# Turning the feed-forward rows in 32x32 blocks on VectorE, by way of DRAM, instead of on TensorE

## The chip, the cores and the metric

The kernel runs on one core of one Trainium2 chip, all in 32-bit floats. The metric is the device time of one execution in microseconds (us), as the median of several runs. TensorE is called PE, its weight loads PEld, VectorE DVE, ScalarE ACT, GpSimd POOL and SyncE SP, as in the profile.

## The reference

The kernel computes one decoder layer on x of [16 batches, 128 tokens, 1024 channels]: a self-attention, a cross-attention on a context, and a gated feed-forward, each on normalised rows and each added to x.

```python
x = x + attn(layernorm(x), Wqkv, bqkv, Wo, bo)            # single head, d = 256
x = x + xattn(layernorm(x), ctx, ctx, Wq, Wk, Wv, Wo, ...)  # 8 heads of 64
Wg, Wu, Wd = (dequantize(...) for each of gate, up, down)  # 4-bit, groups of 64
g = einsum('bsh,ih->bsi', ln, Wg)      # ln = layernorm(x), i < 2752
u = einsum('bsh,ih->bsi', ln, Wu)
x = x + einsum('bsi,hi->bsh', silu(g) * u, Wd)
```

In the feed-forward the contraction runs over the 1024 channels, so TensorE needs the normalised rows turned: channels on the partitions, tokens along the free axis.

## The kernel before

**Stages.** The program runs in four stages that overlap at their borders: the self-attention with the first part of the weight preparation, the cross-attention (one batch after another, batches 8 to 15 and then 0 to 7), the gate and up products with the rest of the weight preparation, and the down products. The products of the feed-forward are Winograd-like: a 2x2 split of tokens, inputs and outputs is done with seven products instead of eight (GATE, DOWN), at two levels for some of them (`two_levels`). The combinations that this needs are made by VectorE (right operands) and GpSimd (left operands).

**Order.** `InOrder` (L54-62) keeps the instructions of an engine in the order in which they are written; `tensor` and `vector` (L529) are such wrappers, so that from the cross-attention on PE and VectorE run in program order, with L62 as the line of all their instructions. ScalarE and the SP queue are ordered by the framework's scheduler, unless a call is wrapped. In the cross-attention, work is put off with `later(n, fn)` and released by `tick()` (L602-612), which is called after each key unit and each query unit: eight ticks to a batch. When the last batch is reached, the ticks go on between the first products of the feed-forward (`beside`, L1502).

**A batch of the cross-attention** (L879-903) is four pairs of a key unit and a query unit. Both fill a PSUM tile kq from a pool of two (`bpk`, L589), which ScalarE's exponential frees for keys (ke, L666) and VectorE's subtraction for queries (qe). The keys' exponentials are already turned in 32x32 blocks by VectorE (kt, L676), written to DRAM (kd, L680) and loaded again with the blocks in place (kh, L684); the product mm<-kh,cxt (L734) reads them as a right operand in runs of 32 values. `project_out` (L789) adds the result to X[b], and `turned(b)` (L771) then normalises the rows for the feed-forward, in two halves n of 512 columns (even and odd channels), into two tiles xn3.

**The turn.** Two ticks later `turn_rows` (L557) turns each half with four 128x128 PE transposes into a PSUM tile tr (pool `btr`, two tiles, shared with the queries' transposes), ScalarE copies it to a tile xt [128, 4, 128], and SP writes xt to DRAM, to `xt_all[pass][n, half]`, laid out [128 partitions, 4 channel groups j, 512 tokens]. Here `half` is which four of a pass's eight batches it is.

**The blocks.** `block_loads` (L541) loads each of the four blocks (n, half) of a pass, [128, 4, 512], in two DMAs of 512 KB, each two j for all tokens. The loads of the first pass are issued by ticks after batch 15 was turned (L783-787), those of the second between products of the feed-forward (L1517). `operand` (L847) and `outer_operand` (L1061) make the combined blocks T[q] from them. A product reads the j-th channel group as `T[q][:, j, :]`, 512 columns without a gap (L1095, L1172); the two-level products read 256 columns of it or of a combination `ti` (L1246-1271, L1326).

Of the kernel before, what the change touches and what calls it, by code (L numbers as in the profile page):

```python
# [11 lines left out]
F32 = mybir.dt.float32  # L12
# [53 lines left out]
def decoder_layer(  # L66
# [467 lines left out]


    PASSES = (HB, 0)
    xt_all = [dram.tile([2, 2, P, JC, TB], F32, name=f"xt{p}", tag=f"xt{p}") for p in range(2)]
    x_all = dram.tile([B, P, C], F32, name="x_all", tag="x_all")
    blocks = {}

    def block_loads(p, blocks):  # L541

        for k in ((0, 0), (1, 0), (1, 1), (0, 1)):
            for i in range(2):
                part = slice(None), ts(i, JC // 2)
                tc.keep_in_program_order(nc.sync.dma_start(blocks[k][part], xt_all[p][k][part]))
                yield

    def new_blocks(pool, tag):

        return {
            (n, half): pool.tile([P, JC, TB], F32, name=f"b{n}{half}", tag=tag(2 * n + half))
            for n in range(2)
            for half in range(2)
        }

    def turn_rows(b, xns, psum, pool):  # L557
        half, i = divmod(b % HB, BPT)
        for n, xn in enumerate(xns):
            tr = psum.tile([P, JC, P], F32, name="tr")  # L560
            for j in range(JC):
                tensor.transpose(tr[:, j, :], xn[:, ts(j, P)], ident)
            xt = pool.tile([P, JC, S], F32, name="xt")
            nc.scalar.copy(xt, tr)
            nc.sync.dma_start(xt_all[PASSES.index(b - b % HB)][n, half][:, :, ts(i, S)], xt)

# [45 lines left out]
    if True:  # L614
# [155 lines left out]

        def turned(b):  # L771

            xns = []
            for n in range(2):
                xn = b2.tile([P, C // 2], F32, name="xn3")

                rows = X[b].rearrange("p (g j e n) -> p n j g e", g=16, j=JC, n=2)[:, n]
                dst = xn.rearrange("p (j g e) -> p j g e", j=JC, g=16)
                normalise_act(dst, rows, b)
                xns.append(xn)  # L780
            nc.gpsimd.dma_start(x_all[b], X[b])
            later(2, lambda: turn_rows(b, xns, btr, b2))
            if b == B - 1:  # L783
                blocks.update(new_blocks(xlate, lambda k: f"X{HB + 2 * k}"))
                loads = block_loads(0, blocks)
                for n in range(8):
                    later(7 + 2 * n, lambda: next(loads))
# [59 lines left out]
        def operand(q):  # L847

            b12 = blocks[0, 1]
            if q == 7:  # L850
                T0[7] = b12
                vector.tensor_tensor(b12, blocks[1, 1], b12, ALU.subtract)
                return
            t = T0[q] = xres.tile(
                [P, JC, TB], F32, name=f"T{q}", tag={5: "X0", 6: "X2", 4: "X4"}[q]
            )
            a, b = {
                5: (b12, blocks[0, 0]),
                6: (blocks[1, 1], T0.get(5)),
                4: (blocks[1, 0], T0.get(6)),  # L860
            }[q]
            vector.tensor_tensor(t, a, b, ALU.subtract)
# [100 lines left out]
    with ExitStack() as gs:  # L963
# [97 lines left out]
        def outer_operand(T, q):  # L1061

            b12 = blocks[0, 1]
            if q == 7:
                vector.tensor_tensor(b12, T[3], b12, ALU.subtract)
                T[7] = b12
                return
            pool, tag = {5: (cxb, "b4"), 6: (xres, "X2"), 4: (xres, "X0")}[q]
            t = T[q] = pool.tile([P, JC, TB], F32, name=f"T{q}", tag=tag)
            a, b = {5: (b12, T[1]), 6: (T[3], T.get(5)), 4: (T[2], T.get(6))}[q]  # L1070
            vector.tensor_tensor(t, a, b, ALU.subtract)

# [2 lines left out]
        def products(T, got, tensor=tensor):  # L1075

            bank, kept = {}, {}

            def keep(q, ps):
                t = kept[q] = ct.tile([P, TB], F32, name="k", tag=f"k{q}", bufs=2 if q == 1 else 1)  # L1080
                nc.scalar.copy(t, ps)

            def product(q):
                wt = next_weights()
                put_stores()
                first = {6: 1, 5: 1, 3: 1, 4: 7}.get(q, q)
                if first == q:
                    banks.rotate(1)
                    bank[q] = banks[0].tile([P, TB], F32, name=f"p{q}", tag="gu")
                ps = bank[first]  # L1090
                for j in range(JC):
                    tensor.matmul(  # L1092
                        ps,
                        wt[:, j, :],
                        T[q][:, j, :],  # L1095
                        start=(first == q and j == 0),
                        stop=(q in (2, 3, 4) and j == JC - 1),
                        skip_group_check=True,
                    )
                if q in (1, 7, 6):  # L1100
                    keep(q, ps)
                elif q == 2:
                    got((0, 0), ps, kept[1])
                elif q == 5:
                    got((1, 1), ps, kept[7])
                elif q == 4:
                    got((1, 0), ps, kept[6])
                elif q == 3:
                    got((0, 1), ps, None)

            return product
# [30 lines left out]
        def last_block(ps, T, between):  # L1142
# [24 lines left out]
            def half_product(p, w, q, start, stop):  # L1167
                for j in range(JC):
                    tensor.matmul(
                        bank[p],  # L1170
                        w[:, j, :],
                        T[q][:, j, :],  # L1172
                        start=(start and j == 0),
                        stop=(stop and j == JC - 1),
                        skip_group_check=True,
                    )
# [57 lines left out]
        class Operands:  # L1234
# [5 lines left out]
            def inner_right(self, q):  # L1240

                R = self.R
                if q in self.kept and (q, 7) in R:
                    return []

                def t(kc, h):  # L1246
                    return self.T[q][:, ts(kc, CHUNKS), ts(h, HT)]

                R[q, 1], R[q, 2], R[q, 3] = t(0, 0), t(1, 0), t(1, 1)

                def comb(k):
                    if k == 7:
                        tag = self.kept.get(q, "ti")
                        pool = {"ti": self.pool, "X4": xres}.get(tag, xlate)
                        R[q] = pool.tile(
                            [P, 4, CHUNKS, HT],
                            F32,
                            name="ti",
                            tag=tag,
                            bufs=1 if self.kept else 2,  # L1260
                        )
                    dst = R[q, k] = R[q][:, (5, 6, 7, 4).index(k)]
                    a, b = {
                        5: (t(0, 1), t(0, 0)),
                        6: (t(1, 1), R.get((q, 5))),
                        7: (t(1, 1), t(0, 1)),
                        4: (t(1, 0), R.get((q, 6))),
                    }[k]
                    vector.tensor_tensor(dst, a, b, ALU.subtract)

                return [lambda k=k: comb(k) for k in (7, 5, 6, 4)]
# [23 lines left out]
        def two_levels(ps, pairs, operands, between=lambda q: None):  # L1295
# [18 lines left out]
            def multiply(n, p):  # L1314
                L, bank = state[n]["L"], state[n]["bank"]
                q = OUTERS[n][1]
                set_ = {6: 1, 5: 1, 3: 1, 4: 7}.get(p, p)
                if set_ == p:
                    bank[p] = banks[n % 2].tile([P, 2, HT], F32, name=f"q{p}", tag="gu")
                dst = bank[set_]  # L1320
                for m in range(2):
                    for c in range(CHUNKS):
                        tensor.matmul(
                            dst[:, m, :],
                            L[p][:, m, c, :],
                            R[q, p][:, c, :],  # L1326

                            start=(set_ == p and m == c == 0),
                            stop=(p in (2, 3, 4) and c == CHUNKS - 1),
                            skip_group_check=True,  # L1330
                        )
                if p in (1, 7, 6):
                    t = state[n]["kept"][p] = ct.tile(
                        [P, 2, HT], F32, name="k", tag=f"k{p}", bufs=2 if p == 1 else 1
                    )
                    scalar.copy(t, dst)
                put_stores()
# [492 lines left out]
```

## Time and profile before

| | |
|---|---|
| time, median of 3 runs | 2290.3 us (2287.9 to 2293.0) |
| time of the profiled execution | 2287.6 us |
| its span in the profile | 2285.8 us |
| busy: PE, DVE, ACT, POOL | 2258.2, 1600.1, 560.0, 471.8 us |
| DMA traffic | 425.23 MB, 270319 packets |
| granted PE clock | 1.00 in all stretches |

By stage, from the view of busy time by stretch (PE, DVE and ACT busy, and the share of the 16 DMA engines):

| us from the span's start | what | PE | DVE | ACT | DMA |
|---|---|---|---|---|---|
| 0 to 252 | self-attention | 241.4 | 197.3 | 37.8 | 0.49 |
| 252 to 806 | cross-attention | 546.5 | 465.6 | 324.4 | 0.62 |
| 806 to 873 | its last batches beside the first products | 66.2 | 22.5 | 36.0 | 0.55 |
| 873 to 1809 | gate and up products | 932.0 | 672.0 | 153.1 | 0.65 |
| 1809 to 2286 | down products | 472.1 | 242.7 | 8.7 | 0.48 |

A line of the groups names the line of the code, the engine, the operation, output<-inputs with their sizes and the count, then the busy time in us and the mean in ns of one, and the idle time of the engine before it. The names are the tiles' names: xn is the normalised rows, tr the PSUM tile of a PE transpose, xt both the turned tile and its place in DRAM, kt and kd the turned keys and their place, kh their load, kq the PSUM tile of key and query units, b a loaded block, T and ti combinations of blocks, w and li left operands, p and q the PSUM tiles of products at one level and at two. In the order of time, a line has its start and its length in us, and in brackets the idle time before it and what ended it. Consecutive matmuls overlap, so that the sum of their lengths is more than the time that they take.

### The profile page before, as it was taken

The page shows a single profiled execution, that of the slowest core. Times are in us where ns is not written, and L with a number is a line of the kernel's source. Part 1 is how long each engine was busy: PE and PEld are TensorE (multiplying, and loading weights), DVE is VectorE, ACT ScalarE, POOL GpSimd, SP SyncE. Part 2 cuts the span into 40 slices and gives each one's busy share as a digit, 9 for nine tenths or more (in the row PEclk, how much of TensorE's full clock was granted, in tenths as well). Part 3 has the DMA queues.
Part 4 walks back from the last instruction along what each step waited for, and adds up shares of the span by engine and source line. Part 5 has one row for each costly group of instructions (what it writes and reads, how often), then busy time and mean ns, then how long its engine had stood idle before and what let it go on. Part 6 is the DMA issues. An engine that isn't in the chain of part 4 may idle for free.

```text
span 2285.8 us, 25587 instructions
## 1 busy us (share of the span) xinstructions
PE 2258.2 (99%) x9096; PEld 1612.5 (71%) x9096; DVE 1600.1 (70%) x2145; ACT 560.0 (24%) x893; POOL 471.8 (21%) x381
## 2 busy tenths in 40 slices
PE   8999999999999999999999999999999999999999
PEld 7556566666666664444584468888888588888888
DVE  6997788788788937666696658877777555544463
ACT  2111255665665652111111111121111100000000
POOL 5452122222222210000240024444443000000000
PEclk9999999999999999999999999999999999999999
DMA  6445366566676558877747942654554974434631
GB/s 246 158 135 182 102 166 183 158 194 185 173 230 196 169 165 269 276 261 262 242 137 232 322 137 95 202 185 139 192 196 137 331 242 151 142 124 149 222 116 37
DMA packets 270319, 425.23 MB, mean 186 GB/s; under 512 B 26224, under 2 KB 119792, under 8 KB 270064
## 3 DMA queue, kind: packets, MB, share of 16 engines
q1 hardware_dynamic: 244112, 377.71, 52.3%
q0 software_dynamic: 8064, 27.27, 3.2%
q10 hardware_dynamic: 18016, 18.62, 2.6%
q8 instruction: 73, 1.20, 0.2%
q14 instruction: 54, 0.44, 0.1%
HBM read 265.62 MB, written 157.35 MB: 185 GB/s over the span
## 4 chain that ended last, share of the span: by engine, by line
PE 91%; DVE 5%; issue 1%; DMA 1%; ACT 1%; POOL 0%; SPq 0%; DVEq 0%; POOLq 0%; ACTq 0%
PE po L1715 21%; PE q L62 20%; PE p L62 18%; PE mm L62 11%; PE kq L62 9%; PE mm L391 4%; PE tr L62 3%; PE mm L406 2%; PE p L1092 2%; DVE pa L62 1%; PE mm L287 1%; PE tr L338 1%; DVE ti L62 0%; DVE bnst L62 0%; DMA kh<-kd 0%
## 5 line engine op out<-in xcount | busy, mean ns | idle before, releaser
L62 PE MATMUL p<-b,w 128*128 128x512 f32 x560 | 246.4, 592 | 0.0
L62 PE MATMUL q<-ti,li 128*128 128x256 f32 x1008 | 232.2, 379 | 3.5 <-DVE ti L62 3.4
L62 PEld LDWEIGHTS q<-ti,li 128*128 128x128 f32 x1008 | 191.0, 190 | 31.3 <-issue 2.8
L62 POOL TENSOR_TENSOR li<-w 128x512 f32<-128x512 f32 x84 | 117.8, 1405 | 432.2 <-DMA w<-wu 244.4
L62 PEld LDWEIGHTS p<-b,w 128*128 128x128 f32 x560 | 106.4, 190 | 133.1 <-issue 129.4
L1715 PE MATMUL po<-wc,lc 128*128 128x256 f32 x840 | 183.4, 379 | 0.0
L62 PE MATMUL p<-T,w 128*128 128x512 f32 x400 | 177.2, 592 | 0.0
L709 POOL TENSOR_TENSOR qe<-qe,qden 128x1024 f32<-128x1024 f32 x64 | 121.7, 1901 | 266.5 <-DVE qden L62 244.7
L1715 PEld LDWEIGHTS po<-wc,lc 128*128 128x128 f32 x840 | 159.6, 190 | 21.8
L62 ACT COPY k<-q 128x512 f32<-128x512 f32 x126 | 73.7, 585 | 400.0 <-PE q L62 400.0
L62 PEld LDWEIGHTS p<-T,w 128*128 128x128 f32 x400 | 76.0, 190 | 95.7 <-issue 94.9
L1715 PE MATMUL po<-wq,lq 128*128 128x256 f32 x560 | 126.7, 379 | 0.4 <-issue 0.4
L62 PE MATMUL mm<-kh,cxt 128*128 128x256 f32 x512 | 122.6, 382 | 3.2 <-DMA kh<-kd 2.8
L62 PEld LDWEIGHTS mm<-qs,m_sb 128*128 128x128 f32 x512 | 97.2, 190 | 38.9 <-issue 28.0
L62 PE MATMUL kq<-cx,wk_sb 128*128 128x512 f32 x256 | 120.7, 594 | 3.5 <-ACT ke L666 3.5
L62 DVE TENSOR_REDUCE qmx<-kq 128x16 f32<-128x1024 f32 x64 | 76.3, 1193 | 63.8 <-PE kq L62 63.8
L62 PE MATMUL kq<-wq_sb,xn 128*128 128x512 f32 x256 | 120.4, 593 | 0.0
L62 PE MATMUL mm<-qs,m_sb 128*128 128x256 f32 x512 | 120.3, 379 | 0.0
L62 PEld LDWEIGHTS mm<-kh,cxt 128*128 128x128 f32 x512 | 95.9, 190 | 33.5 <-issue 19.1
L1715 PEld LDWEIGHTS po<-wq,lq 128*128 128x128 f32 x560 | 106.0, 190 | 16.0 <-issue 1.0
L62 DVE TENSOR_TENSOR pa<-pa,sz 128x1024 f32<-128x1024 int32 x86 | 114.6, 1333 | 2.5
L391 PE MATMUL mm<-xnT,wqkv_sb 128*128 128x512 f32 (+1 forms) x320 | 113.4, 511 | 0.0
(193 smaller groups left out, 3886.1 us busy)
## 6 DMA issues: line engine op xcount, KB each, us to landing
w<-wu SPq DMA_DIRECT2D x140, 256.0 KB, 3.1
lq<-h SPq DMA_DIRECT2D x140, 256.0 KB, 4.3
w<-wg SPq DMA_DIRECT2D x138, 256.0 KB, 2.8
kd<-kt SPq DMA_DIRECT2D x64, 512.0 KB, 3.5
kh<-kd SPq DMA_DIRECT2D x128, 256.0 KB, 5.6
h<-hc SPq DMA_DIRECT2D x80, 256.0 KB, 2.8
wq<-wd SPq DMA_DIRECT2D x70, 256.0 KB, 5.0
h<-h SPq DMA_DIRECT2D x60, 256.0 KB, 2.5
```

The lines of the kernel that those rows point to most:

```text
L62: return lambda *args, **kw: self._tc.keep_in_program_order(fn(*args, **kw))
L287: tensor.matmul(ps, oT[:, d, ts(b % BPT, S)], wo_d[d][:, ts(h, 512)], start=(d == 0), stop=(d == 1),)
L338: nc.tensor.transpose(tr[:, j, :], xn[:, ts(4 * h + j, P)], ident)
L391: nc.tensor.matmul(ps[:, tokens], wqkv_sb[:, f, c, :], xnT[:, c, tokens], start=(c == 0), stop=(c == CC - 1),)
L406: nc.tensor.matmul(ps, xnT[:, c, ts(i, S)], wqkv_sb[:, 4:6, c, :], start=(c == 0), stop=(c == CC - 1),)
L709: nc.gpsimd.tensor_tensor(qe, qe, den.unsqueeze(2).to_broadcast(wide), ALU.mult)
L1092: tensor.matmul(ps, wt[:, j, :], T[q][:, j, :], start=(first == q and j == 0), stop=(q in (2, 3, 4) and j == JC - 1), skip_group_check=True,)
L1715: nc.tensor.matmul(bank[:, i, :], l[:, ts(i, S)], w,  start=(start and c == 0 and i % 2 == 0), stop=(stop and c == len(pairs) - 1), skip_g ...
```

## The change

The 16 calls of `turn_rows` no longer use PE and ScalarE. The normalised rows of a batch go into one tile xn3 [128, 8, 128] (both halves n), VectorE turns it with one instruction in 32x32 blocks into a tile xt of [128, 4, 8, 32], and four DMAs, one for each group of 32 partitions, write it to DRAM; block c of the rows' columns belongs on partitions 32c to 32c+31, which the DMA from DRAM brings about. `xt_all` has another layout: by batch, token group a, column block c, partition i, and then contiguous (n, j, 32 tokens).

A block is now [128, 16 token groups, 4 channel groups j, 32 tokens] instead of [128, 4, 512]. Its loads are still two of 512 KB, each now eight token groups with all four j, in contiguous pieces of (j, 32 tokens). All that reads a block or a combination, at one level and at two, takes the j-th channel group as 16 (or 8) runs of 32 tokens.

```diff
     PASSES = (HB, 0)
-    xt_all = [dram.tile([2, 2, P, JC, TB], F32, name=f"xt{p}", tag=f"xt{p}") for p in range(2)]
+    xt_all = [
+        dram.tile([HB, 4, 4, Q, 2, JC, Q], F32, name=f"xt{p}", tag=f"xt{p}") for p in range(2)
+    ]
...
+    TOKENS = TB // Q
...
     def block_loads(p, blocks):
-        for k in ((0, 0), (1, 0), (1, 1), (0, 1)):
+        for n, half in ((0, 0), (1, 0), (1, 1), (0, 1)):
             for i in range(2):
-                part = slice(None), ts(i, JC // 2)
-                tc.keep_in_program_order(nc.sync.dma_start(blocks[k][part], xt_all[p][k][part]))
+                src = xt_all[p][ds(half * BPT + 2 * i, 2), :, :, :, n]
+                tc.keep_in_program_order(
+                    nc.sync.dma_start(
+                        blocks[n, half][:, ts(i, TOKENS // 2)],
+                        src.rearrange("b a c i j t -> (c i) (b a) j t"),
+                    )
+                )
                 yield
     def new_blocks(pool, tag):
         return {
-            (n, half): pool.tile([P, JC, TB], F32, name=f"b{n}{half}", tag=tag(2 * n + half))
+            (n, half): pool.tile([P, TOKENS, JC, Q], F32, name=f"b{n}{half}", tag=tag(2 * n + half))
...
-    def turn_rows(b, xns, psum, pool):
-        half, i = divmod(b % HB, BPT)
-        for n, xn in enumerate(xns):
-            tr = psum.tile([P, JC, P], F32, name="tr")
-            for j in range(JC):
-                tensor.transpose(tr[:, j, :], xn[:, ts(j, P)], ident)
-            xt = pool.tile([P, JC, S], F32, name="xt")
-            nc.scalar.copy(xt, tr)
-            nc.sync.dma_start(xt_all[PASSES.index(b - b % HB)][n, half][:, :, ts(i, S)], xt)
+    def turn_rows(b, xn, pool):
+        kt = pool.tile([P, 4, 2 * JC, Q], F32, name="xt")
+        vector.transpose(
+            kt.rearrange("p c m t -> p m c t"), xn.rearrange("p m (c i) -> p m c i", c=4)
+        )
+        xt = xt_all[PASSES.index(b - b % HB)][b % HB]
+        for a in range(4):
+            nc.sync.dma_start(
+                xt[a].rearrange("c i n j t -> i c (n j t)"),
+                kt[ts(a, Q)].rearrange("i c m t -> i c (m t)"),
+            )
...
         def turned(b):
-            xns = []
+            xn = b1.tile([P, 2 * JC, P], F32, name="xn3")
             for n in range(2):
-                xn = b2.tile([P, C // 2], F32, name="xn3")
                 rows = X[b].rearrange("p (g j e n) -> p n j g e", g=16, j=JC, n=2)[:, n]
-                dst = xn.rearrange("p (j g e) -> p j g e", j=JC, g=16)
+                dst = xn[:, ts(n, JC)].rearrange("p j (g e) -> p j g e", g=16)
                 normalise_act(dst, rows, b)
-                xns.append(xn)
             nc.gpsimd.dma_start(x_all[b], X[b])
-            later(2, lambda: turn_rows(b, xns, btr, b2))
+            later(2, lambda: turn_rows(b, xn, b1))
...
-                [P, JC, TB], F32, name=f"T{q}", tag={5: "X0", 6: "X2", 4: "X4"}[q]
+                [P, TOKENS, JC, Q], F32, name=f"T{q}", tag={5: "X0", 6: "X2", 4: "X4"}[q]
...
-                        T[q][:, j, :],
+                        T[q][:, :, j],
...
-                    return self.T[q][:, ts(kc, CHUNKS), ts(h, HT)]
+                    return self.T[q][:, ts(h, HT // Q), ts(kc, CHUNKS)]
...
-                            [P, 4, CHUNKS, HT],
+                            [P, 4, HT // Q, CHUNKS, Q],
...
-                            R[q, p][:, c, :],
+                            R[q, p][:, :, c],
```

The line `T[q][:, :, j]` stands in both kinds of one-level product, and the tile of `outer_operand` has the same new shape.

More of the change, by code (lines that the diff above doesn't have):

```diff
@@ L1068, in outer_operand @@
             pool, tag = {5: (cxb, "b4"), 6: (xres, "X2"), 4: (xres, "X0")}[q]
-            t = T[q] = pool.tile([P, JC, TB], F32, name=f"T{q}", tag=tag)
+            t = T[q] = pool.tile([P, TOKENS, JC, Q], F32, name=f"T{q}", tag=tag)
             a, b = {5: (b12, T[1]), 6: (T[3], T.get(5)), 4: (T[2], T.get(6))}[q]
@@ L1171, in half_product @@
                         w[:, j, :],
-                        T[q][:, j, :],
+                        T[q][:, :, j],
                         start=(start and j == 0),
```

## The prediction, made before the changed kernel was run

> **What bounds the kernel now.** I read the busy shares and the chain of waits first, to learn which engine sets the end:
>
> ```profile
> PE 2258.2 (99%) x9096; PEld 1612.5 (71%) x9096; DVE 1600.1 (70%) x2145; ACT 560.0 (24%) x893; POOL 471.8 (21%) x381
> PE 91%; DVE 5%; issue 1%; DMA 1%; ACT 1%; POOL 0%; SPq 0%; DVEq 0%; POOLq 0%; ACTq 0%
> ```
>
> TensorE (PE) holds 91% of the chain. A busy PE isn't one at its peak, so next come the stretches in which the change works: one period of the cross-attention, a fuller one, and the stretch where the second half's blocks are loaded.
>
> ```profile
> 425.00:460.00 35.00, 35.00 (x158) 24.04 (x157) 29.12 (x36) 21.48 (x37) 8.79 (x6) 1.00 0.62 179
> 740.00:775.00 35.00, 35.00 (x160) 24.04 (x159) 33.00 (x37) 21.34 (x34) 8.79 (x6) 1.00 0.61 178
> 1220.00:1310.00 90.00, 90.00 (x211) 39.77 (x211) 56.42 (x80) 10.79 (x19) 0.00 (x0) 1.00 1.00 305
> ```
>
> (Columns: PE, PEld, DVE, ACT, POOL busy, granted clock, DMA share, GB/s.) PE has no gap in any of them; VectorE has 5.9 us of 35 free in the first, 2.0 in the second; the DMA engines are full in the third. Then the groups removed or to be copied from:
>
> ```profile
> L62 PE MATMUL tr<-ident,xn 128*128 128x128 f32 x128 | 16.8, 273 | 0.1
> L564 ACT COPY xt<-tr 128x512 f32<-128x512 f32 x32 | 18.4, 584 | 1.0
> L62 DVE STREAM_TRANSPOSE kt<-ke 128x1024 f32<-128x1024 f32 x64 | 79.2, 1237 | 0.0
> ```
>
> Last, the order of time around one turn:
>
> ```profile
> 506.79 1.89 PE L62 MATMUL mm<-qs,m_sb 128*128 128x256 f32 x8
> 508.51 1.89 PE L62 MATMUL mm<-kh,cxt 128*128 128x256 f32 x8
> ...
> 512.83 1.89 PE L62 MATMUL mm<-kh,cxt 128*128 128x256 f32 x8
> ...
> 514.29 1.23 DVE L62 TENSOR_TENSOR qe<-kq,qmx 128x1024 f32<-128x1024 f32 x1
> ...
> 514.56 1.04 PE L62 MATMUL tr<-ident,xn 128*128 128x128 f32 x8
> ...
> 515.43 1.88 PE L62 MATMUL kq<-cx,wk_sb 128*128 128x512 f32 x4
> 515.43 1.24 DVE L62 STREAM_TRANSPOSE kt<-ke 128x1024 f32<-128x1024 f32 x1
> ...
> 517.35 1.22 DVE L62 TENSOR_REDUCE knmax<-kq 128x1 f32<-128x1024 f32 x1 [0.68 <-PE kq L62]
> ...
> 521.66 1.23 DVE L62 TENSOR_REDUCE qmx<-kq 128x16 f32<-128x1024 f32 x1 [1.67 <-PE kq L62]
> ```
>
> Durations overlap on PE, so its price is from start to start: the eight transposes hold it from 514.56 to 515.43, 0.87 us, or 0.109 us each, not the 273 ns of the group. VectorE's two gaps end when PE delivers.
>
> **What the skill says.** (1) "TensorE: Matmul & The Clock Gate", Part 4: PE-mode transpose: some 275 ns in a kernel's context, and a copy out of PSUM after. The record here agrees (273 ns), but the spacing is 109 ns; I use the spacing. (2) "VectorE: DVE Perf Modes", The three transpose paths: VectorE turns 32x32 blocks only, within SBUF. Hence the way through DRAM. Our trace has the operation, at 1.237 us for 128x1024. (3) "SBUF — State Buffer", Who interferes with whom: a VectorE instruction with one SBUF input, outside the two-port modes, doesn't contend with GpSimd. The 64 key transposes of before agree: 1233 to 1246 ns, whatever GpSimd does beside them. (4) "DMA: Bandwidth & Descriptors", Specifications: line rate from 512 B on. The trace roughly agrees: xt<-xt writes 512 B runs, 256 KB landing in 2.9 us, beside 2.8 to 3.1 us for the w loads with 2 KB runs.
>
> **The change part by part.**
>
> *Removed from PE:* 8 transposes x 16 batches = 128 x 0.109 = 13.9 us. They lie in stretches where PE has no gap, so all of it is on the path: -13.9.
>
> *Removed from ScalarE:* 32 copies x 0.584 = 18.7 us. ScalarE is 61% busy in the period (21.48 of 35), behind PE: 0.
>
> *Added on VectorE:* 16 transposes x 1.237 = 19.8 us. Per period its work goes from 29.1 to 30.4 us while the period shrinks from 34.86 (515.43 less 480.57, the same product a batch earlier) to 33.99. It fits, but VectorE runs in program order, so I follow the tick. The new transpose would run after qe, from 515.5 to 516.7, and the key transpose to 518.0. knmax then starts 0.6 us later than before, ScalarE's exponential ends near 520.4, and with it the PSUM buffer of this key unit comes free. The key unit that reuses it is two units on, at 524.4 (489.55 plus a period), now 523.5: 3 us of slack. By the next qmx (now due at 520.8) VectorE has caught up, since the gap of 1.67 us absorbs the rest. Cost 0 in 15 batches. In the batch with two T operands VectorE has 33.0+1.24 = 34.2 us in 34: I put 0.3 us on it; ends 0 and 1.2 (the whole transpose shows).
>
> *New waits:* the transpose waits for ScalarE's normalised rows on VectorE, and knmax, qden and the next qmx queue behind it; those rows are made two ticks ahead (504.15 to 505.7 for a turn at 514.6), so nothing is waited for. One xn3 and one xt buffer instead of two half-size ones: each is reused a batch later, tens of us. The SP queue waits for VectorE instead of ScalarE.
>
> *SP queue:* four stores per batch instead of two, 2 x 0.52 = 1.04 us more, behind a transpose that ends 1 us or so after the last copy did. The key store (517.81) queues behind and slips by up to 2 us; its loads come 12 us later (530.3). Cost 0.
>
> *DMA:* two windows give a price by packet size: 320 to 600 us, 36059 packets, 46.13 MB, 58.4% of 16 engines = 72.6 ns at 1279 B; 1216 to 1310, 13679 packets, 28.49 MB, 99.2% = 109 ns at 2083 B. So an estimate of 14.6 ns + 45 ns per 1000 B: 38 ns for 512 B, 200 ns for 4 KB. A block load of 512 KB had 128 pieces of 4 KB, 1.6 us on 16 engines; with 1024 pieces of 512 B it is 2.4. The stores gain: 1 KB pieces, half as many. The 8 loads of the first half are issued from 641 to 702 us, and the first use of the last is at 720, so they have time; but one kh load there already holds PE for 2.6 us. The 8 loads of the second half (1216 to 1290) add 8 x 0.8 = 6.5 us of work where the share is 1.00. PE doesn't wait for DMA there: weights are asked for four tiles, about 13.8 us of products, ahead and land in 5 to 7. But VectorE's weight preparation does (one wait of 8.0 us for a store). Bounds: -2.6 (the kh stall goes) to +6.5; I take +0.5.
>
> *Right operands by blocks of 32 tokens:* the product reads runs of 32 values, 128 B, with a stride. 1072 products of 512 columns and 2352 of 256 do so; in passes of 256 that is 4496. The trace has the case: mm<-kh,cxt reads runs of 32 too, and eight take 1.73 us (512.83 to 514.56) against 1.72 for the contiguous mm<-qs,m_sb (506.79 to 508.51). Cost 0; the upper end is 0.01/8 = 1.25 ns per pass, 5.6 us. A gain is excluded, as contiguous already runs at the full spacing. VectorE's combinations of these operands keep their element counts; kt<-ke writes runs of 32 at the speed of a contiguous 128x1024 (1.22 to 1.23): 0.
>
> *Sum:* -13.9 + 0.3 + 0.5 = -13.1. On the profiled execution (span 2285.8, 2287.6 with what lies around) 2274.5; the median of the runs, 2290.3, lies 2.7 above it, so 2277.2; I say 2277.
>
> **What is next.** PE stays the bound. In the fuller period VectorE is level with it, and a further VectorE task there would show.
>
> **The rivals.**
> (a) *The gain is partly given back to the DMA engines.* For: share 1.00 from 1220 to 1310, 0.82 around 690 with a kh stall. Against: no PE wait at 1.00. The 6.5 us in full, after 0.3 elsewhere: 2290.3 - 13.9 + 6.8 = 2283.
> (b) *VectorE's order becomes the bound in the cross-attention.* If each transpose pushed PE by 0.87 or more per batch, the gain is gone: 2290. For: 30.4 of 34 us, in order, with waits on PE in between. Against: 740 to 775, where 33.0 of 35 on VectorE left PE without a gap.
> (c) *Slower: strided reads of the right operand.* Should PE read runs of 32 more slowly with 16 runs than with 8, each pass pays. It decides from 13.9 / 4496 = 3.1 ns per pass, 1.4% of 0.216 us; at 6 ns it is 27 us, 2303. For: the means of the two groups stand at 382 and 379 ns. Against: their medians are both 379, and the spacing.
> (d) *PE's time in the tail doesn't follow*, because the transposes there fill waits for ScalarE; three of 16 batches, 2.6 us: inside the range.
>
> **How the numbers follow.** Likeliest (full gain) 0.72, (a) 0.14, (b) 0.07, (c) 0.07. The likeliest's own range is 2272 to 2281 (the kh stall gone or VectorE's and part of the DMA cost). For 8 in 10 the range takes in (a): 2272 to 2287; (b), (c) and some of the low end stay out. About 0.2%, 4.6 us, can be told from no change here: faster means below 2285.7. That is the likeliest, and most of (a): 0.83; same: (b) and a rest of (a), 0.09; slower: (c) and a little of (b), 0.08.
>
> **What would show it.** Right: period of the cross-attention 34.0 us from one kq<-cx to the same a batch on; tr<-ident,xn and xt<-tr gone; VectorE near 30.4 per period; p and q product spacing as before (0.43 and 0.216 us). Wrong: PE waits for ke or qe between 320 and 800 (b); PE or VectorE waits on DMA growing at 690 or 1220 to 1310 (a); q<-ti,li or p<-T,w means above 379 and 592 ns (c). Unequal order on the SP queue could shift single stalls by some us either way.

## The result, and the profile after

| | before | after |
|---|---|---|
| median of the runs | 2289.1 us (4 runs) | 2273.2 us (2272.05 to 2274.74, 4 runs) |
| ratio to before | 1 | 0.9927 [0.9914, 0.9939] |
| profiled execution, its span | 2287.6, 2285.8 us | 2272.22, 2270.4 us |
| busy: PE, DVE, ACT, POOL | 2258.2, 1600.1, 560.0, 471.8 us | 2243.3, 1616.5, 546.2, 473.7 us |

The change is faster by 0.7%. On 2290 us the ratio is 16.7 us, between 14.0 and 19.7; my sum was 13.1 and the forecast 2277. In a later session it came to 0.9924 [0.9911, 0.9936].

The page of the changed kernel, engines and chain of waits:

```profile
PE 2243.3 (99%) x8968; PEld 1598.7 (70%) x8968; DVE 1616.5 (71%) x2161; ACT 546.2 (24%) x861; POOL 473.7 (21%) x381
PE 91%; DVE 6%; issue 2%; DMA 1%; ACT 1%; POOL 0%; SPq 0%; DVEq 0%; POOLq 0%; ACTq 0%
```

PE lost 14.9 us of busy time and is still 91% of the chain: the bound hasn't moved. Now the stretches (the columns are those of the prediction). The first line is one whole period of the cross-attention, from a key unit's first product to the same product a batch later; the second is the fullest one, in which VectorE also makes two T operands; the third is where the second half's blocks are loaded. Then the period of before.

```profile
477.26:511.25 33.99, 33.99 (x150) 23.07 (x149) 29.99 (x36) 20.50 (x32) 8.79 (x6) 1.00 0.67 190
724.15:758.14 33.99, 33.99 (x150) 23.08 (x148) 32.87 (x35) 20.34 (x32) 7.74 (x6) 1.00 0.63 186
1200.00:1320.00 120.00, 120.00 (x281) 53.03 (x280) 80.76 (x107) 15.37 (x26) 1.21 (x1) 1.00 0.92 280
```

```profile
480.57:515.43 34.86, 34.86 (x158) 23.90 (x157) 28.98 (x35) 21.32 (x35) 8.78 (x6) 1.00 0.61 181
```

PE is busy through all of them. VectorE has 30.0 us of work in a period of 33.99 (29.0 of 34.86 before, the last line, between the starts that the prediction names), and in the fullest 32.9 of 33.99. The DMA share in the third is 0.92 over the whole 120 us, and no PE gap goes with it. The groups:

```profile
L62 PE MATMUL p<-b,w 128*128 128x512 f32 x560 | 246.4, 592 | 0.0
L62 PE MATMUL q<-ti,li 128*128 128x256 f32 x1008 | 232.2, 379 | 3.5 <-DVE ti L62 2.8 <-ACT k L62 0.6
L62 DVE STREAM_TRANSPOSE kt<-ke 128x1024 f32<-128x1024 f32 x64 | 78.7, 1230 | 0.3 <-issue 0.3
L62 DVE STREAM_TRANSPOSE xt<-xn 128x1024 f32<-128x1024 f32 x16 | 19.8, 1234 | 1.0 <-ACT xn L147 1.0
```

`tr<-ident,xn` and `xt<-tr` are gone; in their place stand 16 VectorE transposes at 1234 ns. The products that now read runs of 32 tokens still take 592 and 379 ns, as these lines of before have it:

```profile
L62 PE MATMUL p<-b,w 128*128 128x512 f32 x560 | 246.4, 592 | 0.0
L62 PE MATMUL q<-ti,li 128*128 128x256 f32 x1008 | 232.2, 379 | 3.5 <-DVE ti L62 3.4
```

Their spacing is the old one too: between the 201st and the 561st product of 512 columns the traces have 154.50 us in both kernels. The order of time around a turn:

```profile
477.26 1.88 PE L62 MATMUL kq<-cx,wk_sb 128*128 128x512 f32 x4
...
511.25 1.88 PE L62 MATMUL kq<-cx,wk_sb 128*128 128x512 f32 x4
...
512.12 1.23 DVE L62 STREAM_TRANSPOSE xt<-xn 128x1024 f32<-128x1024 f32 x1
...
513.28 1.20 DVE L62 STREAM_TRANSPOSE kt<-ke 128x1024 f32<-128x1024 f32 x1
...
514.41 1.18 DVE L62 TENSOR_REDUCE knmax<-kq 128x1 f32<-128x1024 f32 x1
...
517.47 1.23 DVE L62 TENSOR_REDUCE qmx<-kq 128x16 f32<-128x1024 f32 x1 [0.47 <-PE kq L62]
```

From the first line to the second is one batch: 33.99 us. The lines of before had 480.57 to 515.43, 34.86. VectorE does the new turn at 512.12, then the keys', and knmax starts 3.2 us after the key unit's first product, 1.9 us before. By the next qmx it has caught up: its gap there is 0.47 us instead of 1.67. This is the tick as I had followed it. (The prediction's 0.6 us for knmax is on the clock of before; from a key unit that itself starts 0.87 us sooner that is 1.5 us later, and 1.2 was measured.)

One long wait is gone that the sum took as likely to stay. PE's waits for the load kh, in total us, times and longest, before and after:

```profile
PE mm L62 <- DMA kh<-kd: 2.8, 2, 2.6
```

```profile
PE mm L62 <- DMA kh<-kd: 0.2, 1, 0.2
```

The wait of 2.6 us is gone; the 0.2 that is left, at 302 us, is in both. The reason is the subject of experiment 3.

### The profile page after: what moved, and what is told of

It is laid out like the page before. It is cut to its first block, busy times and chain, and to the rows that moved or that the text cites. A ratio compares the mean times of both kernels' runs of the same rounds, so it can differ in the third digit from the quotient of the medians.

```text
span 2270.4 us, 25324 instructions
## 1 busy us (share of the span) xinstructions
PE 2243.3 (99%) x8968; PEld 1598.7 (70%) x8968; DVE 1616.5 (71%) x2161; ACT 546.2 (24%) x861; POOL 473.7 (21%) x381
## 4 chain that ended last, share of the span: by engine, by line
PE 91%; DVE 6%; issue 2%; DMA 1%; ACT 1%; POOL 0%; SPq 0%; DVEq 0%; POOLq 0%; ACTq 0%
PE po L1725 21%; PE q L62 20%; PE p L62 18%; PE mm L62 11%; PE kq L62 8%; PE mm L391 4%; PE tr L62 2%; PE p L1102 2%; PE mm L406 2%; DVE pa L62 1%; PE mm L287 1%; PE tr L338 1%; DVE ti L62 0%; DVE bnst L62 0%; DVE kt L62 0%
```

## The experiments

All ratios are to the kernel before, timed in turn with it on the same chip. The changed kernel stands at 0.9927, and at 0.9924 in a later session.

**1. PE's turns put back.** The changed kernel, with the eight transposes of each batch also on PE, into a PSUM tile that nobody reads.

```diff
     def turn_rows(b, xn, pool):
         kt = pool.tile([P, 4, 2 * JC, Q], F32, name="xt")
+        for n in range(2):
+            tr = btr.tile([P, JC, P], F32, name="tr")
+            for j in range(JC):
+                tensor.transpose(tr[:, j, :], xn[:, JC * n + j], ident)
         vector.transpose(
```

> The changed kernel with the eight 128x128 PE transposes of each batch put back beside VectorE's (their PSUM tile is read by nobody; no ScalarE copy). My theory (the gain is PE's spacing, 0.109 us a transpose, on a path without gaps): 128 x 0.109 = 13.9 us more than the changed kernel, 2273.2 + 13.9 = 2287, and a period of the cross-attention of 34.86 us instead of 33.98. Rival 1 (the gain comes from ScalarE's copies and its freer queue, or from the other DMA sizes): within 3 us of the changed kernel, 2273 to 2276. Rival 2 (PE pays the 273 ns of the record): 35 us more, 2308.

Measured: 2286.3 us, 0.9984 [0.9977, 0.9992]. That is 0.0057 to 0.0060 above the changed kernel, 13.1 to 13.7 us, with some 3.5 us of uncertainty from the two intervals. The period, from a key unit's first product to the next batch's:

```profile
482.67 1.88 PE L62 MATMUL kq<-cx,wk_sb 128*128 128x512 f32 x4
...
517.53 1.88 PE L62 MATMUL kq<-cx,wk_sb 128*128 128x512 f32 x4
```

34.86 us, the period of before to 0.01 us. So eight transposes take 0.87 us of PE, and neither the copies that ScalarE no longer does nor the other stores have a part in it, for here too the copies are away and the stores are the new ones. The 273 ns of the record would have made 35 us. But this kernel is still faster than before by 0.8 to 2.3 parts in a thousand: something else had been gained.

**2. The layout alone.** The turn as before, on PE and ScalarE, with the blocks, their loads and the right operands of the changed kernel.

```diff
-        kt = pool.tile([P, 4, 2 * JC, Q], F32, name="xt")
-        vector.transpose(
-            kt.rearrange("p c m t -> p m c t"), xn.rearrange("p m (c i) -> p m c i", c=4)
-        )
+        kt = pool.tile([P, 4, 2, JC, Q], F32, name="xt")
+        for n in range(2):
+            tr = btr.tile([P, JC, P], F32, name="tr")
+            for j in range(JC):
+                tensor.transpose(tr[:, j, :], xn[:, JC * n + j], ident)
+            nc.scalar.copy(kt[:, :, n].rearrange("p a j t -> p j a t"),
+                           tr.rearrange("p j (a t) -> p j a t", a=4))
         for a in range(4):
-            nc.sync.dma_start(xt[a].rearrange("c i n j t -> i c (n j t)"), ...)
+            nc.sync.dma_start(xt[a].rearrange("c i n j t -> (c i) (n j t)"), ...)
```

> The turn as before (eight PE transposes, ScalarE's copies), with the new layout of blocks in DRAM and SBUF, its loads in pieces of 512 B, its four stores a batch and the right operands in runs of 32 tokens. My theory: the layout costs PE nothing; means of the product groups stay at 592 and 379 ns, time as the kernel before within 3 us (2286 to 2290, the lower end if the one kh stall of 2.6 us goes). Rival (c) of the prediction (strided reads cost PE): 2295 or more with a wider spacing of the products. Rival (a) (pieces of 512 B cost): up to 6.5 us more, 2292 to 2296, with PE or VectorE waiting on DMA from 1220 to 1320 us.

Measured: 2290.6 us, 0.9999 [0.9991, 1.0007]. No cost to within 2 us, and the groups say the same:

```profile
L62 PE MATMUL p<-b,w 128*128 128x512 f32 x560 | 246.4, 592 | 0.0
L62 PE MATMUL q<-ti,li 128*128 128x256 f32 x1008 | 233.7, 381 | 3.5 <-DVE ti L62 2.8 <-ACT k L62 0.6
```

Runs of 32 tokens, 128 B, are read at the speed of a contiguous operand, also when there are 16 of them. The slower rival (c) is refuted. In this run a kh wait of 2.0 us is still there: the layout isn't what took it away.

**3. One cxt load moved.** In the kernel before, the scheduler had put the load of a context tile ahead of four kh loads on the SP queue:

```profile
689.07 0.33 SPq L654 DMA_DIRECT2D cxt<-in_cxt  x1
689.51 1.80 SPq L684 DMA_DIRECT2D kh<-kd  x4
...
699.53 1.97 PE L62 MATMUL mm<-kh,cxt 128*128 128x256 f32 x8 [2.56 <-DMA kh<-kd]
```

The waits of the SP queue name what held it:

```profile
SPq L654 <- PE mm L62: 6.6, 1, 6.6
```

The cxt load couldn't start until PE had read a buffer, and held the queue 6.6 us for it; kh came 2.56 us too late for PE. In the changed kernel's queue, cxt stands behind kh there:

```profile
677.74 1.75 SPq L696 DMA_DIRECT2D kh<-kd  x4
...
693.27 0.93 SPq L666 DMA_DIRECT2D cxt<-in_cxt  x1
```

The edit gives the kernel before this order. The traces show what else moved with it: one block load, which stood at 701.83 ahead of the next four kh loads, now stands behind them as in the changed kernel, and ScalarE makes one copy xt<-tr 2.4 us earlier, at 726. Both come after the stall. All else on the SP queue, PE, VectorE and GpSimd has the same order.

```diff
-            nc.sync.dma_start(ct, cxt[b])
+            d = nc.sync.dma_start(ct, cxt[b])
+            if b == 6:
+                tc.keep_in_program_order(d)
...
-                        nc.sync.dma_start(
-                            t[ts(c, Q)], kd[:, :, c].rearrange("p i o n j -> i p o n j")
-                        )
+                        tc.keep_in_program_order(nc.sync.dma_start(...))
```

> The kernel before with one load of the SP queue moved: the context tile cxt of batch 6 is issued behind the four kh loads that it stood ahead of, nothing else. My theory (the 2.6 us by which the change beat my forecast are this one stall, made by the scheduler's order of the SP queue and not by the change's own work): the PE wait of 2.56 us on kh at 697 us goes and the time falls by 2.6, to 0.9989 of the kernel before. Rival (the stall is made by the DMA engines' load around 690, whatever the order): the wait stays, no change of time.

Measured: 2286.1 us, 0.9982 [0.9976, 0.9989], 4.1 us less (2.5 to 5.5), with 21 runs against 45. The wait:

```profile
PE mm L62 <- DMA kh<-kd: 0.4, 1, 0.4
```

The wait of 2.6 us is gone, as expected (the 0.4 is another, at 304 us, which the kernel before has with 0.2). The middle of the timed gain is 1.5 us more, and the granted clock fits it. Over the 45 runs of the kernel before it has a mean of 0.9985, over these 21 runs 0.9994, and 0.0009 of 2286 us is 2 us. The two kernels that keep the stall, before and experiment 2, both have 0.9985; experiments 1 and 3 and the changed kernel, which lack it, have 0.9994 to 0.9995. (The versions of experiments 4 to 6, which wait longer at the border to the feed-forward, lie between 0.9980 and 0.9990.) Compared at the same listed clock, this version is 2.3 to 2.8 us faster, which is the wait. The split is an estimate from the clocks listed for the runs; that the stall brings the lower clock about isn't shown by a run of its own. The trace of experiment 2 shows how the two may hang together. There PE's wait for kh ends at 699.21, after 2.0 us, and then comes a stretch at half clock:

```profile
699.65:703.05 3.40, 3.40 (x9) 2.40 (x8) 2.28 (x3) 0.23 (x1) 0.00 (x0) 0.50 1.11 367
```

3.4 us at half the clock are 1.7 us of work lost. It doesn't follow every such wait: the profiled execution of the kernel before went on at 1.00 after its 2.56 us. (The profiled execution here has a span of 2285.6 us, only 0.2 below the one of before, because it started the cross-attention 0.8 us later and had 3.4 us at half clock from 1202.5, behind another PE wait of 2.4 us, where the one of before had none.)

The remainder of experiment 1 is the same size: it too has the changed kernel's order. Experiment 2 has the old one, so it is the new turn, and not the layout, that the scheduler answered with another order. So the change's gain has two parts, 13 to 14 us of PE work and some 4 us of queue order with what follows from it; together about 17.5, beside the 16.7 measured.

**4. More turns on VectorE.** The changed kernel, with each batch's transpose done twice, or four times, into the same tile:

```diff
-        vector.transpose(
-            kt.rearrange("p c m t -> p m c t"), xn.rearrange("p m (c i) -> p m c i", c=4)
-        )
+        for _ in range(2):  # 4 in the second
+            vector.transpose(
+                kt.rearrange("p c m t -> p m c t"), xn.rearrange("p m (c i) -> p m c i", c=4)
+            )
```

> The changed kernel with VectorE's transpose of each batch done twice into the same tile (16 x 1.234 = 19.7 us more on VectorE). My theory: VectorE has 31.6 of 33.98 us in a period, still fits, and PE doesn't wait: the changed kernel within 2 us, 2273 to 2275. Rival (b) of the prediction (VectorE's order binds in the cross-attention already): each of 16 turns shows, 2285 to 2293.

Measured: 2277.9 us, 0.9944 [0.9932, 0.9957]: 3.9 us above the changed kernel, though the intervals touch. The expected upper end was 2. A period:

```profile
476.72:510.71 33.99, 33.99 (x150) 23.03 (x149) 31.17 (x37) 20.61 (x32) 8.78 (x6) 1.00 0.67 193
```

33.99 us as before, with VectorE at 31.2: in the steady stretch another 1.2 us cost nothing, so my theory holds there. The excess lies at the late end of the cross-attention: PE waits 4.8 us for ke instead of 3.7, the new gaps being at 766 and 775 us, behind a period with two T operands in which VectorE was busy for 33.4 of 33.99 us; and it waits 3.0 for the first weights w<-wg instead of 1.7. Behind this last wait stand 3.4 us at half clock, from 797.3, which neither profiled execution of the changed kernel has.

> The changed kernel with VectorE's transpose of each batch done four times into the same tile (16 x 3 x 1.234 = 59 us more on VectorE). My theory: VectorE's work in a period is 30.4 + 3.7 = 34.1 us, more than PE's 33.98, and it still has a gap or two waiting on PE, so that here it becomes the bound: a period of 34.5 to 36 us, 8 to 30 us more than the changed kernel, 2281 to 2303, with PE waiting for ScalarE's ke. If VectorE had hidden slack (rival: its program order costs nothing at all until the sum is over the period) only 2 us: 2275.

Measured: 2308.3 us, 1.0081 [1.0067, 1.0094], 35 us above the changed kernel, more than expected. A period, and PE's wait over the whole run:

```profile
475.24:511.38 36.14, 34.79 (x149) 22.80 (x149) 33.58 (x39) 20.79 (x33) 8.78 (x6) 1.00 0.60 172
```

```profile
PE kq L62 <- ACT ke L679: 20.7, 28, 1.6
```

The period is 36.14 us, 2.15 more. VectorE is busy for 33.6 of it, 93%, and PE has gaps that end with ke. So rival (b) is a real mechanism, at a load that the change doesn't reach: the changed kernel is at 30.0 of 33.99, 88%. The share alone doesn't set the point: experiment 6 runs at 94%, batch after batch, with no PE gap. Here all four transposes lie in one piece of 5.07 us ahead of the keys' transpose and knmax, and knmax starts 7.0 us after its key unit's first product, where the changed kernel has 3.2: 3.8 us later, against the 3 us of slack that the prediction counted for the PSUM tile. And VectorE, in program order, still waits for PE once in the period (1.9 us for qmx). Whether the long piece or the sum of the work sets the period wasn't separated.

**5. Loads of 4 KB again.** The changed kernel with `xt_all` laid out [pass][n, half, partition, batch, token group, j, 32]: loads in pieces of 4 KB, eight stores a batch in pieces of 512 B.

```diff
-        dram.tile([HB, 4, 4, Q, 2, JC, Q], F32, ...)
+        dram.tile([2, 2, P, BPT, 4, JC, Q], F32, ...)
...
-                src = xt_all[p][ds(half * BPT + 2 * i, 2), :, :, :, n]
+                src = xt_all[p][n, half, :, ds(2 * i, 2)]
...
         for a in range(4):
-            nc.sync.dma_start(
-                xt[a].rearrange("c i n j t -> i c (n j t)"),
-                kt[ts(a, Q)].rearrange("i c m t -> i c (m t)"),
-            )
+            for n in range(2):
+                nc.sync.dma_start(
+                    xt[n, half, :, i, a].rearrange("(c i) j t -> i c (j t)", c=4),
+                    kt[ts(a, Q), :, ts(n, JC)].rearrange("i c m t -> i c (m t)"),
+                )
```

> The changed kernel with another layout of the turned rows in DRAM: the block loads read pieces of 4 KB again, and the stores write pieces of 512 B (eight of them a batch instead of four). SBUF and the products stay as in the changed kernel. My theory: the pieces of 512 B cost some 6 us of DMA work from 1200 to 1320 us and nothing on the path, so the time stays within 2 us of the changed kernel (2271 to 2275) while the DMA share in that stretch falls. Rival (a) (they cost on the path): 3 to 6.5 us faster than the changed kernel.

Measured: 2276.7 us, 0.9941 [0.9927, 0.9955]: not faster than the changed kernel, rather 3 us slower, with intervals that overlap. Rival (a) is refuted: nothing was waiting on the pieces of 512 B. The stretch of the block loads:

```profile
1200.00:1320.00 120.00, 120.00 (x281) 53.19 (x280) 79.77 (x109) 16.23 (x27) 0.00 (x0) 1.00 0.91 276
```

A share of 0.91 where the changed kernel has 0.92. I had expected it to fall by some 6 us of 120, which is 0.05. My price by packet size was wrong at its upper end. In the packet records of these two traces, from 1200 to 1320 us, a piece of 512 B takes 34 ns on average, near my 38, but one of 4 KB takes 272 to 281, where I had 200; eight small ones cost as much as one large one. A block load lands after 6.3 us in the median in both, as before the change.

That this version isn't as fast as the changed one is mostly the granted clock: it has a mean of 0.9984 over the five runs, against 0.9995 and 0.9994, which is some 2.4 us. Its profiled execution, 2.0 us longer than the changed kernel's, has 3.4 us at half clock from 253.6, ahead of all that the edit touches. Why the clock was lower in these runs stays open.

**6. The same trick once more.** With 4 us of VectorE free in a steady period, one of the four query units of a batch can be turned that way too: one VectorE transpose, four stores, and a load two ticks later, in the layout of `xt`; the product reads `qs` in runs of 32. First in all batches, then in the third to eleventh, then in the third to thirteenth.

```diff
+            def turn_by_dram():
+                qd = dram.tile([4, 4, Q, 8 * Q], F32, name="qd", tag="qd", bufs=2)
+                qt = bqs.tile([P, 4, 2, 4, Q], F32, name="qs", tag="qs")
+                qs.append(qt.rearrange("p a i r t -> p r i a t"))
+                kt = bkt.tile([P, 4, NB, Q], F32, name="kt")
+                vector.transpose(kt.rearrange("p c m t -> p m c t"),
+                    qe.rearrange("p h d -> p (h d)").rearrange("p (m c y) -> p m c y", c=4, y=Q))
+                for a in range(4):
+                    nc.sync.dma_start(qd[a].rearrange("c y x -> y c x"),
+                                      kt[ts(a, Q)].rearrange("y c m t -> y c (m t)"))
+                later(2, lambda: nc.sync.dma_start(qt.rearrange("p a i r t -> p a (i r t)"),
+                                                   qd.rearrange("a c y x -> (c y) a x")))
...
-            later(4, turn)
+            later(4, turn_by_dram if by_dram else turn)
```

Here `by_dram` is pair 0 of every batch in the first version, and pair 0 of the batches named in the two others.

> The changed kernel, in which one of a batch's four query units is also turned by VectorE in 32x32 blocks and by way of DRAM (one transpose, four stores, one load), instead of by eight PE transposes and two ScalarE copies. It takes another 128 transposes from PE: -13.9 us. VectorE then has 31.6 us in a period of 33.1. The run with one more vector turn came out 3.9 us above the changed kernel, so some of it shows: I expect 4 to 8 us back, 2263 to 2269, faster than the changed kernel. Rival (VectorE's order binds, or kh loads now wait behind the new stores on the SP queue): 2273 or more, with PE waiting for ke, kh or qs.

Measured: 2270.2 us, 0.9913 [0.99, 0.9925], 3 us below the changed kernel, though the intervals overlap: less than expected. Where the other 11 of 13.9 us went is seen by stretch. First the changed kernel, its start and the border to the feed-forward, then this one, with a period between:

```profile
252.00:320.00 68.00, 63.03 (x227) 34.19 (x225) 60.38 (x76) 29.49 (x44) 15.52 (x11) 1.00 0.46 130
785.00:806.00 21.00, 19.34 (x87) 12.50 (x86) 18.02 (x21) 10.66 (x17) 6.04 (x6) 1.00 0.85 245
```

```profile
252.00:320.00 68.00, 59.16 (x196) 30.30 (x195) 60.74 (x76) 27.75 (x40) 15.50 (x11) 1.00 0.56 163
466.74:499.85 33.11, 33.11 (x141) 22.25 (x140) 31.11 (x37) 19.62 (x31) 8.77 (x7) 1.00 0.78 223
785.00:806.00 21.00, 17.97 (x59) 11.58 (x60) 10.00 (x12) 5.51 (x10) 3.01 (x3) 0.84 0.93 283
```

The period is 33.11 us, 0.88 less again, with VectorE at 31.1 (94% of it): in the middle the trick pays in full. But PE has 59.2 us of work in the first 68, where it had 63.0; the third batch starts at 318.8 us instead of 316.3, although 1.7 us of transposes are gone from the two ahead of it, and VectorE still has the last of the self-attention there. And at the border PE has 18.0 of 21, at a granted clock of 0.84: a wait of 3.7 us for the first weights, which ends at 788.0, and 6.8 us at half clock, from 786.6. Hence the second version:

> As the run with one query unit by DRAM, but only in the third to eleventh of the 16 batches, where VectorE has the room; in the first two (which also finish the self-attention) and in the last five (block loads, T operands, the border to the feed-forward) the unit is turned on PE as in the changed kernel. Where the loss of the full version lay at the two ends (my theory), the nine units give their 9 x 8 x 0.109 = 7.8 us in full: 2265 where the changed kernel has 2273. Where the loss is spread over all batches (rival), about half of the full version's gain: 2271 or more.

Measured: 2265.8 us, 0.9891 [0.9876, 0.9906], 7.0 us below the changed kernel in the same session; 7.8 was the full gain of nine units. The rival's 2271 is excluded: the loss lay at the ends.

> The same in the third to thirteenth batch: two more units in the batches that also load the blocks, 9.6 us less than the changed kernel if they too come free: 2263.6; 1 to 3 us more than that if the loads from 640 to 705 us then hold up kh (theory), so 2264 to 2267.

Measured: 2264.8 us, 0.9888 [0.9874, 0.9901]; 8.0 us below the changed kernel, of 9.6. The stretches:

```profile
252.00:320.00 68.00, 62.02 (x218) 33.30 (x216) 59.68 (x75) 29.85 (x44) 15.50 (x11) 1.00 0.45 132
640.00:705.00 65.00, 65.00 (x282) 43.88 (x281) 61.33 (x72) 39.82 (x61) 16.57 (x12) 1.00 1.00 277
785.00:806.00 21.00, 20.30 (x70) 13.10 (x70) 10.16 (x12) 6.59 (x11) 3.01 (x3) 0.92 0.86 262
```

The start is nearly that of the changed kernel again, and PE has no gap from 640 to 705 although the DMA share there is 1.00. The 0.92 at the border is 3.4 us at half clock from 786.4, behind a PE wait of 1.9 us for the first weights that ends at 785.7. This is the fastest kernel of the study. It can't be told from the version with nine units.

> The changed kernel once more, beside the two others and the kernel before on one chip, so that the differences of a few us have a base: 0.993 of the kernel before.

Measured: 2272.8 us, 0.9924 [0.9911, 0.9936].

## Why the prediction was right

*Removed from PE, -13.9.* Right. Experiment 1 gives 13.1 to 13.7, with 3.5 us of uncertainty, and the period is 0.87 us shorter. What made it right is taking the spacing (0.109 us) and not the record (0.273), and having read that PE has no gap where the transposes lay.

*Removed from ScalarE, 0.* Right: in experiment 1 ScalarE's copies stay away and the period is that of before.

*Added on VectorE, 0.3.* Right in size: no PE gap in the period or in the fullest one, and one new gap of 0.18 us behind it, at 774.0, that ends with ke. Experiment 4 shows how near the edge is: a second transpose is free in the steady batches, and three more aren't.

*New waits, SP queue, 0.* Right in the cross-attention. The four stores don't even take the 1.04 us more that I had counted: 1.75 us of the queue, where the two of before took 1.95. But one wait at the border was put at nothing without a reason: PE waits 1.7 us for the first weights, w<-wg, in both executions of the changed kernel, and 0.7 before and 0.8 in experiment 1, where it still makes the transposes. It gets there 12 us sooner than before, at 794.4 instead of 806.8, and 1.0 us more of that goes in the wait. The wait of 1.4 instead of 0.3 us for a weight at 251 us lies ahead of anything that was changed (0.3 again in the later session).

*Right operands by 32 tokens, 0.* Right, with experiment 2's bound of 2 us. The evidence had been in the trace of before, in mm<-kh,cxt.

*DMA, +0.5 between -2.6 and +6.5.* This is the term that was mis-sized: -4.1 was measured, more than the 3.6 us between 13.1 and 16.7. I took the kh stall as likely to stay, as a matter of the load on the DMA engines, and put a small cost on the pieces of 512 B. The stall was one of order: a cxt load that waited for PE in front of kh on the SP queue. The changed kernel's queue has another order there, and experiment 3 has the effect by itself, 4.1 us (2.5 to 5.5), of which 2.6 are the wait; the rest fits the granted clock, which was lower where the stall was. The profiled executions of before and after, both at a clock of 1.00, differ by 15.4 us. The pieces of 512 B cost nothing that shows (experiment 5); the straight line through two mean packet sizes gave the pieces of 4 KB too low a price. That the scheduler would order that queue differently couldn't be read from the profile of before; that the stall was one of order could: the line of SP at 689.07 stood in it, with its wait for PE, and the DMA engines had a share of only 0.46 from 685 to 695 us, while kh was late. That the new order fell out in the change's favour was luck. The range took it in by its bound of -2.6, and the prediction's last line, that order on the SP queue could shift single stalls, is what happened.

The rivals: (a) is refuted by experiment 5, (c) by experiment 2; (b) is a mechanism of this kernel, but sets in at a VectorE load that the change doesn't reach. (d) didn't show: 13.1 to 13.7 of 13.9 us came through, and what PE lost at the border it lost to the weights.

## What to carry to other kernels

Where PE is the bound with no gaps, price its work by the distance from start to start, and move to another engine what that engine can turn in a period, in pieces short enough that what PE waits for next isn't late: here pieces of 1.2 us were free at 94% of the period, batch after batch, and a piece of 5 us at 93% wasn't. The next such move is measured first by doing the added instruction twice. Look at the stretch, not the kernel: the same move paid 0.88 us a batch in the middle and cost PE gaps at both ends, so it was made only in the middle. And a change of any kind can reorder a DMA queue that a scheduler fills: find the few long waits behind such a queue and test the order by itself, before a gain of a few us is put down to the change. Where a few us are at stake, compare runs at the same granted clock too.

## What the runs showed of the hardware that I had not expected

VectorE in program order held PE up with 33.6 us of work in 36.14, when four transposes came in one piece; in single pieces 31.1 in 33.11 held up nothing. Block loads in pieces of 512 B (16 x 512 KB) were no slower on the path than in pieces of 4 KB, and the DMA share over their stretch was the same, 0.92 and 0.91: 34 ns for a piece of 512 B, 272 to 281 for one of 4 KB.

A PE wait of some 2 us may cost more than itself. The granted clock fell to one half for 3.4 us, 1.7 us of work, behind PE waits of 1.98 (experiment 2), 1.90 (the last version) and 3.0 us (the second transpose), and for 6.8 us around one of 3.7 (the query unit in all batches). It stayed at 1.00 behind waits of 1.66 and 1.74 (the changed kernel, both executions), but also behind 2.0 (experiment 5, at the border) and 2.56 (before). Behind one wait that all versions have, 2.1 to 2.4 us for ti at the block loads, it fell in 7 of the 12 profiled executions, and of the two of the changed kernel in one. So the length of the wait alone doesn't decide it; what does stays open.
